# Tables of the first batch group in two passes: keys first, then values from a second reading of x, with joint rows moved to the second group and a new order

## Chip, core and metric

The kernel runs on one core of a Trainium2 chip. The metric is device time in microseconds. The kernel before was run nine times: median 2289.28 us, lowest 2274.66, highest 2302.47. The profile comes from one further execution of 2278.17 us. The engines are TensorE (PE, matrix products and transposes), VectorE (DVE), ScalarE (ACT), GpSimd (POOL, which also issues the indirect DMAs: gathers and scatters by row index) and SyncE (SP, which issues the plain DMAs in its queue's order).

## What is computed

Two graph layers over x (8 batches, 2048 nodes, 256 features) with one adjacency matrix (2048 x 2048, about 5 to 24 neighbours a row). Layer 0 is attention with 4 heads over the neighbours, with a softmax in each chunk of 256 nodes, then two normalizations. Layer 1 is graph attention with a softmax over all neighbours. Cut to what matters:

```python
q, k, v = (x @ W.T + b for each of Wq, Wk, Wv)            # 4 heads of 64
scores = clip(einsum('bhnd,bhjcd->bhnjc', q, kc) / 8, -10, 10)   # j: 8 chunks of 256 nodes
scores = where(mask == 0, -10, scores)
attn = softmax(scores, axis=-1)                            # within each chunk
ctx = einsum('bhnjc,bhjcd->bhnd', attn, vc)
x = layernorm(x + layernorm(ctx @ Wo.T + bo + x) * gamma + beta)
Wh = x @ W                                                 # layer 1
e = leaky_relu(s_src + s_dst); alpha = softmax(where(adj, e, -inf))
x = layernorm(x + elu(alpha @ Wh))
```

Since masked neighbours keep a weight of exp(-10) in each chunk, the kernel subtracts the chunk's mean of x before the value product ("centring"), so that the masked part becomes a constant that is added elsewhere. That is why values need the sum over a chunk of x, and keys do not.

## The kernel before, in words

**Sparse path.** Nodes are sorted by degree into 16 tiles of 128 nodes. Tile t has CAPS[t] neighbour slots (24, 14, 13, 12, 11, 11, 10, 10, 9, 9, 8, 8, 7, 7, 6, 5: 164 in all). The 8 batches are two groups of 4 (p = 0 and 1, "first" and "second"). One table row holds a node for all 4 batches of a group: 1024 numbers, 4 KB.

**Lists** (`edge_lists`). The adjacency rows are read, the neighbour numbers of each node are picked (L369, L406 to L412 on DVE), the nodes are ranked by degree (L378 to L397), each record is scattered to its place (L417, 16 indirect DMAs on POOL) and read back in order (L421). The index lists `idx`, `idk` (2 x index) and `idv` (2 x index + 1) are made from it (L429 to L435).

**Tables** (`tables(p, c2, ...)`, 8 chunks of two tiles of 128 nodes for each group). SP loads x (L699, 512 KB), PE transposes it (L682), ACT empties the bank with a running sum into `xs` (L705), POOL (first group) or DVE (second) adds beta (L708), and SP writes that to `xd_d` (L714). Then the chunk's mean is made (L722, L724), x is centred into `xc` (first group: one addition on POOL, L733; second group: 8 activations on ACT, L729), PE makes keys from `xT` and values from `xc` (L742, 32 matmuls of 256 columns a tile), DVE empties the keys with the bias (L747), ACT the values (L752), and SP writes both halves of the row of `kv_d[p]` (L754, L755), an 8 KB row of keys and values. Banks: the first group uses room "n" (two banks), which is given to the attention once the group's tables are done; the second group uses "m" (two banks), which transposes and queries use too. `shifts(p)` makes a constant of the query path from the sums of x (L760 to L789).

**Layer 0** (`layer0(v, p, t)` for each tile and group). `fetch_x` gathers x rows (L934); `query` transposes them (L682, ACT L945) and makes q (L953, L688). Keys are gathered (`gather`, L851, one indirect DMA a slot; two slots share a buffer of the room "u"), multiplied by q on DVE (L972), turned on PE (L985), copied by ACT (L988) and summed by heads on PE (L992), or reduced on DVE (L977) for the few units in `DOTS`. `softmax0` (L1007 to L1026) follows. Values are gathered (L851, by `idv`) and weighed (L894 on DVE for one or two slots at once, or L885 on ACT: 16 activations a slot), and summed by PE (L903). Some slots come as a joint row of key and value (`gather_both`, L864): S % 2 + 2 x COMBO[p] of a tile's S slots. With COMBO = (1, 0) that is 40 slots of the first group and 8 of the second. `apart0` says which slots go to ACT: the first SHARE[S] joint ones. `finish0` does the output product, the normalizations and the rows of layer 1.

**Layer 1** (`layer1`) gathers the new rows (L851), weighs (L894, L885) and sums (L903), for the two groups apart in 8 tiles and jointly in the other 8, and scatters the result (L1183).

**Order.** Every operation is put into a list with its engine, an estimated cost, its reads and writes and a due value v (`pl.stage(lo, hi)` spreads a range over the operations since the last call). When the program is built, `Plan.schedule` plays the list through: whenever an engine is free it takes the ready operation with the least v whose buffers are free. The result is each engine's fixed order; on the chip each engine goes through its own order and waits by semaphores. The due values are constants at the head of the file: WHENT (first value and step by chunk for the second group's tables), FIRST[0:2] the same for the first group's, WHEN0 the offsets of layer 0's steps, ORD0 and ORD1 the place of each tile. In the units of v, tile k of the first group stands at about k. Before, the second group's eight chunks stand at -22.35, -17.3, -12.25, -7.2, -2.15, 2.9, 7.95 and 13.

## Time and profile before

| what | value |
|---|---|
| profiled execution, time / span | 2278.17 us / 2276.4 us |
| PE, PE weight loads, DVE, ACT, POOL busy | 80%, 71%, 78%, 48%, 55% of the span |
| instructions | 36611 |
| DMA | 635.55 MB, mean 279 GB/s |
| gathers and scatters (queue q0) | 505.18 MB, 62.7% of 16 engines' span |
| plain DMAs (queue q1) | 126.24 MB, 15.1% |
| DVE busy by stage: 0 to 201, 201 to 361, 350 to 1000 us | 127.4, 84.2, 538.4 us |
| PE busy by the same stages | 153.7, 132.2, 558.1 us |

How to read the profile: a line of the groups has the source line, engine, operation, what is written and read, the count, then the busy time and mean duration, then the time the engine sat idle just before and what ended it. In a timeline the first two numbers are the start and the duration in us, and the bracket is the idle time before, with what ended it; "issue" is idle time that nothing in the profile explains. The slices on the page cut the span into 40 parts and give the busy share in tenths. The chain of work that ended last reaches back only to 1747 us in this profile; what happens before is read from the stages and the waits.

### The profile page before, as it was taken

What the parts mean: (1) busy time and instruction counts of PE and PEld (TensorE: products, weight loads), DVE (VectorE), ACT (ScalarE), POOL (GpSimd) and SP (SyncE); (2) the same over time, 40 slices, a digit from 0 to 9 for tenths busy, and PEclk for the clock granted to TensorE, in tenths of its full rate; (3) what the DMA queues carried; (4) which work ended last, traced back from release to release, by engine and by line L of the source; (5) the groups of instructions that cost most, each with busy time, mean ns of one, the idle gap of its engine ahead of it and who ended that gap; (6) DMA issues with size and microseconds to landing.
All of it is one profiled execution on the core that took longest, in us unless ns stands there. A gap on an engine that the chain in (4) does not pass through costs nothing. (4 is left out here: it accounts for less than half of the span.)

```text
span 2276.4 us, 36611 instructions
## 1 busy us (share of the span) xinstructions
PE 1819.2 (80%) x12215; PEld 1622.8 (71%) x12215; DVE 1766.6 (78%) x3262; ACT 1101.9 (48%) x4033; POOL 1249.0 (55%) x1192
## 2 busy tenths in 40 slices
PE   5697898788889788888787788888898867755755
PEld 4576788687778677777677777777787666755745
DVE  7922749698879777987777867788878788987987
ACT  6543544165355345441061532434455468664667
POOL 6684126554443434356646655555566565665676
PEclk9898999799989889999899988999999988877967
DMA  8867576898877767669868877888888699987873
GB/s 306 306 239 286 206 287 203 303 339 303 289 276 281 286 243 277 230 222 313 308 235 313 291 273 256 289 294 301 278 302 283 237 338 346 363 319 276 312 241 116
DMA packets 191672, 635.55 MB, mean 279 GB/s; under 512 B 36597, under 2 KB 54903, under 8 KB 178821
## 3 DMA queue, kind: packets, MB, share of 16 engines
q0 software_dynamic: 142160, 505.18, 62.7%
q1 hardware_dynamic: 46608, 126.24, 15.1%
q8 instruction: 99, 1.62, 0.3%
q10 hardware_dynamic: 2708, 1.71, 0.3%
q14 instruction: 97, 0.79, 0.1%
HBM read 596.19 MB, written 109.71 MB: 310 GB/s over the span
## 5 line engine op out<-in xcount | busy, mean ns | idle before, releaser
L903 PE MATMUL acc<-ident,u 128*128 128x128 f32 x2640 | 356.0, 288 | 57.4 <-DVE u L894 37.2
L903 PEld LDWEIGHTS acc<-ident,u 128*128 128x128 f32 x2640 | 321.2, 151 | 70.5 <-DVE u L894 42.6
L894 DVE TENSOR_TENSOR u<-u,h 128x2048 f32<-128x2048 f32 (+1 forms) x176 | 332.7, 1904 | 0.3
L972 DVE TENSOR_TENSOR u<-u,q 128x1024 f32<-128x1024 f32 x241 | 287.0, 1212 | 45.3 <-PE q L688 30.0
L851 POOL DMA_INDIRECT u<-kv_d,idv x194 | 211.2, 1089 | 195.4 <-PE acc L903 67.5
L851 POOL DMA_INDIRECT u<-kv_d,idk x206 | 208.5, 1012 | 193.8 <-issue 43.2
L885 ACT ACTIVATE u<-u,s 128x64 f32<-128x64 f32 x1056 | 261.1, 351 | 10.4 <-DVE s L1149 2.5
L985 PE MATMUL h<-ident,u 128*128 128x128 f32 x1568 | 209.2, 283 | 12.9 <-issue 7.6
L988 ACT COPY h<-h 128x256 f32<-128x256 f32 (+1 forms) x156 | 53.9, 346 | 323.4 <-PE h L985 169.2
L985 PEld LDWEIGHTS h<-ident,u 128*128 128x128 f32 x1568 | 186.7, 148 | 24.0 <-issue 11.4
L1082 PE MATMUL m<-wa,b 128*128 128x264 f32 x512 | 150.7, 430 | 27.7 <-issue 16.7
L821 ACT ACTIVATE b<-b,x,x 128x256 f32<-128x256 f32 x256 | 137.5, 602 | 72.5 <-DVE x L818 52.4
L1183 POOL DMA_INDIRECT out_dram<-b,nodeb x128 | 134.1, 1048 | 66.9 <-issue 28.6
L992 PEld LDWEIGHTS h<-sel,h 128*128 128x128 f32 x546 | 80.0, 202 | 117.1 <-ACT h L988 49.2
L903 PE MATMUL acc<-ident,at 128*128 128x128 f32 x1192 | 152.9, 278 | 8.4 <-issue 5.2
L992 PE MATMUL h<-sel,h 128*128 128x16 f32 x546 | 83.3, 261 | 94.5 <-ACT h L988 38.9
L894 DVE TENSOR_TENSOR at<-at,h 128x2048 f32<-128x2048 f32 (+1 forms) x82 | 154.3, 1890 | 2.3 <-DMA at<-kv_d,idv 2.2
L1052 PE MATMUL m<-wo,b 128*128 128x256 f32 x512 | 137.2, 392 | 20.1 <-issue 12.6
L953 PE MATMUL q<-wq,pair 128*128 128x256 f32 x512 | 140.0, 398 | 11.3 <-ACT pair L945 8.3
L903 PEld LDWEIGHTS acc<-ident,at 128*128 128x128 f32 x1192 | 137.6, 145 | 13.3 <-issue 7.3
L1082 PEld LDWEIGHTS m<-wa,b 128*128 128x128 f32 x512 | 98.2, 209 | 48.0 <-issue 20.4
L972 DVE TENSOR_TENSOR at<-at,q 128x1024 f32<-128x1024 f32 x87 | 103.7, 1212 | 31.0 <-PE q L688 20.5
(232 smaller groups left out, 4239.8 us busy)
## 6 DMA issues: line engine op xcount, KB each, us to landing
kv_d<-b SPq DMA_DIRECT2D x64, 512.0 KB
at<-in_adj_dram SPq DMA_DIRECT2D x16, 1024.0 KB
x_d<-b SPq DMA_DIRECT2D x32, 512.0 KB
b<-x_d SPq DMA_DIRECT2D x32, 512.0 KB
b<-in_x_dram SPq DMA_DIRECT2D x24, 512.0 KB
xd_d<-b SPq DMA_DIRECT2D x24, 512.0 KB
wj_d<-wh_d SPq DMA_DIRECT2D x16, 520.0 KB
at<-in_x_dram SPq DMA_DIRECT2D x8, 512.0 KB
```

The lines of the kernel that those rows point to most:

```text
L821: S(c_act(F, 2), lambda k=k: nc.scalar.activation(batches(dst)[:, k, :], src(k), AF.Identity, scale=rs.t[:, k:k + 1], bias=nm.t[:, k:k + 1 ...
L851: Pq(C_DGE, lambda u=u, o=o, s=s: nc.gpsimd.indirect_dma_start(out=flat(u)[:, o:o + size], out_offset=None, in_=table, in_offset=bass.Indi ...
L885: S(4 * C_WEIGH, lambda u=u, s=s, o=o, c=c, e=e, at=at: [nc.scalar.activation(flat(u)[:, o + h * D:o + (h + 1) * D], flat(u)[:, o + h * D: ...
L894: eng.tensor_tensor(pv, pv, av, op=ALU.mult)
L903: nc.tensor.matmul(quarters(accs[p][c // 4])[:, c % 4, :], flat(u)[:, o + c * P:o + (c + 1) * P], ident, is_transpose=True, start=not done ...
L953: nc.tensor.matmul(qb, cols(xT)[:, (2 * half + b) * KC + kc, :], wq[:, kc, :], start=(b == 0 and kc == 0), stop=False, skip_group_check=True)
L972: V(c_tt(GF), lambda u=u, o=o: nc.vector.tensor_tensor(by_feature(flat(u)[:, o:o + GF], "j b"), by_feature(flat(u)[:, o:o + GF], "j b"), b ...
L985: nc.tensor.matmul(pr.t[:, k * P:(k + 1) * P], flat(u)[:, o + j * P:o + (j + 1) * P], ident, is_transpose=True, start=(j == 0), stop=(j == ...
L992: nc.tensor.matmul(scv(s), prT.t[:, k * P:(k + 1) * P], sel, start=True, stop=True, skip_group_check=True)
L1052: nc.tensor.matmul(ob, cols(cT)[:, b * KC + kc, :], wo[:, kc, :], start=False, stop=(k == 1 and kc == KC - 1), skip_group_check=True)
L1082: nc.tensor.matmul(pw.t[:, 0:F + 2 * H], cols(xT1)[:, b * KC + kc, :], wa[:, kc, :], start=(kc == 0), stop=(kc == KC - 1))
L1183: Pq(C_DGE, lambda b=b: nc.gpsimd.indirect_dma_start(out=out_v[t * B + p * G + b], out_offset=bass.IndirectOffsetOnAxis(ap=nodeb.t[:, t, p ...
```

## The change

For the first group, `tables` now makes only the keys, from `xT`, and writes them to a table of their own, `k_d` (4 KB rows). A new function `again(0, c2)`, queued behind the keys with due values from -13.9 in steps of 0.25, reads x a second time, transposes it again, centres it on ACT while the bank is emptied, makes the values through room "m" and writes them to `v_d`. The chunk means are made on DVE. The second group keeps the joined table `kv_d` and its one pass; its chunks now stand at -4.0, -1.8, 0.4, 2.6, 4.8, 7.0, 9.2 and 11.4. COMBO becomes (0, 1): no joint rows in the first group, S % 2 + 2 in the second (40 slots). SHARE is given for each group, and the slots that go to ACT are the last ones of a tile, joint or not: 35 slots in the first group (29 before) and 11 in the second (7 before). The transposes of `query` now are ordered behind the group's shift. All other due values are new numbers.

```diff
-WHENT = (-22.35, 5.05)
+WHENT = (-4.0, 2.2)
-COMBO = (1, 0)
-SHARE = {5: 0, 6: 0, 7: 2, 8: 2, 9: 2, 10: 2, 11: 2, 12: 2, 13: 3, 14: 4, 24: 4}
+COMBO = (0, 1)
+SHARE = ({5: 0, 6: 0, 7: 3, 8: 2, 9: 3, 10: 2, 11: 3, 12: 2, 13: 3, 14: 2, 24: 2}, {5: 0, 6: 0, 7: 1, 8: 0, 9: 1, 10: 0, 11: 1, 12: 0, 13: 1, 14: 2, 24: 2})
...
-FIRST = (-38.1, 0.5, 2.25, -0.7, -40.65, -31.75, -38.15, -43.75, 4.9)
+FIRST = (-41.05, -0.7, 8.45, -1.45, -39.65, -25.25, -29.75, -38.6, 2.7)
+AGAIN = (-13.9, 0.25)
...
-    kv_d = [nc.dram_tensor(f"kv_d{p}", [N, 2 * GF], F32).ap() for p in range(NP)]
+    kv_d = nc.dram_tensor("kv_d", [N, 2 * GF], F32).ap()
+    k_d, v_d = (nc.dram_tensor(n, [N, GF], F32).ap() for n in ("k_d", "v_d"))
...
-        for t, xT, xc in both:
-            ks, vs = pl.new("b"), pl.new("b")
+        for t, xT in both:
+            keys(p, t, xT)
             if p:
+                xc = pl.new("l")
+                mean = got["mean", p, c2] if t % 2 else chunk_mean(p, c2)
                 for k in range(GK):
...
-            else:
-                Pq(60 + 2.35 * GF, lambda xT=xT, xc=xc: nc.gpsimd.tensor_tensor(
-                    cols(xc), cols(xT), mean.t[:, 0:GK].unsqueeze(2).to_broadcast([P, GK, P]), op=ALU.add), r=[xT, mean],
-                   w=[xc])
...
+                values(p, t, xc)
...
+    def keys(p, t, xT):
+        ks = pl.new("b")
+        project(xT, 0, "m" if p else "n", lambda b, pk: V(c_tt(512), lambda: nc.vector.tensor_tensor(
...
+        Q(lambda: nc.sync.dma_start((kv_d if p else k_d)[t * P:(t + 1) * P, 0:GF], rows(ks)), ROW, r=[ks], loose=[kk_b[p]])
+
+    def values(p, t, xc):
+        vs = pl.new("b")
+        project(xc, 1, "m", lambda b, pv: S(c_act(512), lambda: nc.scalar.copy(vs.t[:, b * F:(b + 2) * F], pv.t), r=[pv],
+                                            w=[(vs, b, b + 2)]))
+        Q(lambda: nc.sync.dma_start(kv_d[t * P:(t + 1) * P, GF:] if p else v_d[t * P:(t + 1) * P, :], rows(vs)), ROW, r=[vs], loose=[kv_b[p]])
+
+    def again(p, c2):
+        mean = chunk_mean(p, c2)
+        for t in (2 * c2, 2 * c2 + 1):
+            xl, xc, gate = pl.new("b"), pl.new("b"), pl.new("gx")
+            Q(lambda t=t, xl=xl: nc.sync.dma_start(batches(xl), x[p * G:(p + 1) * G, t * P:(t + 1) * P, :]
+                                                   .rearrange("b p f -> p b f")), ROW, w=[xl, gate])
+            for half in range(2):
+                pt = turned(xl, half)
+                for c in range(4):
+                    k = 4 * half + c
+                    S(c_act(P, 1), lambda c=c, k=k, pt=pt, xc=xc: nc.scalar.activation(
+                        cols(xc)[:, k, :], quarters(pt)[:, c, :], AF.Identity, bias=mean.t[:, k:k + 1]), r=[pt, mean, gate],
+                      w=[(xc, k, k + 1)])
+            values(p, t, xc)
...
     def apart0(p, t):
-        n = min(SHARE[CAPS[t]], len(got["both", p, t]))
-        return [items[0][0] for _, items in got["both", p, t][:n]]
+        n = SHARE[p][CAPS[t]]
+        return list(range(CAPS[t] - n, CAPS[t]))
...
-            pt = turned(xg, half)
+            pt = turned(xg, half, shift[p])
...
+    for c2 in range(NCH):
+        again(0, c2)
+        pl.stage(AGAIN[0] + c2 * AGAIN[1], AGAIN[0] + (c2 + 1) * AGAIN[1])
...
-        c = S_ - min(S_ % 2 + 2 * COMBO[p], S_)
-        halves_of = kv_d[p].rearrange("n (k f) -> (n k) f", k=2)
-        got["k", p, t] = gather(GF, halves_of, [kv_b[p]], idk, lambda s: idk.t[:, t, s:s + 1], list(range(c)), (p,), WW)
+        c = S_ - min(S_ % 2 + 2 * COMBO[p], S_) if p else S_
+        halves_of = kv_d.rearrange("n (k f) -> (n k) f", k=2)
+        of, at = (halves_of, idk) if p else (k_d, idx)
+        got["k", p, t] = gather(GF, of, [kk_b[p]], at, lambda s, at=at: at.t[:, t, s:s + 1], list(range(c)), (p,), WW)
...
-        got["v", p, t] = gather(GF, halves_of, [kv_b[p]], idv, lambda s: idv.t[:, t, s:s + 1], list(range(c)), (p,), WW)
+        of, at = (halves_of, idv) if p else (v_d, idx)
+        got["v", p, t] = gather(GF, of, [kv_b[p]], at, lambda s, at=at: at.t[:, t, s:s + 1], list(range(c)), (p,), WW)
```

`project(src, part, room, put)` holds the matmuls that stood in `tables` (four a bank, two banks a tile and part), and `chunk_mean` the two small DVE operations.

## The prediction

> **What bounds the kernel now.** I read the page first, then the busy time by stage, then the engines' timelines from 100 to 370 us, then who waited for whom. The page's slices (one is 56.9 us) name the place:
>
> ```profile
> PE   5697898788889788888787788888898867755755
> DVE  7922749698879777987777867788878788987987
> ```
>
> VectorE (DVE) stands nearly idle in slices 3 and 4 (114 to 228 us), while TensorE (PE) is at 80 to 90% there. Nothing like it comes again. The stages, with columns: length, then busy us (instructions) of PE, PE's weight loads, DVE, ACT and POOL, then the granted PE clock, DMA share and GB/s:
>
> ```profile
> 125.00:150.00 25.00, 24.04 (x121) 21.07 (x122) 5.01 (x8) 11.57 (x69) 19.61 (x16) 0.93 0.61 210
> 150.00:175.00 25.00, 25.00 (x125) 22.14 (x124) 5.04 (x8) 7.78 (x38) 22.31 (x24) 1.00 0.80 278
> 175.00:200.00 25.00, 23.94 (x122) 20.69 (x121) 9.22 (x31) 9.20 (x34) 4.58 (x5) 1.00 0.67 241
> 201.00:361.00 160.00, 132.18 (x751) 113.33 (x752) 84.18 (x95) 73.10 (x329) 51.21 (x50) 0.94 0.74 265
> 250.00:300.00 50.00, 47.53 (x273) 41.66 (x272) 33.48 (x37) 21.37 (x101) 9.02 (x9) 0.98 0.58 208
> 350.00:400.00 50.00, 45.91 (x342) 42.78 (x342) 46.41 (x37) 28.16 (x122) 34.91 (x23) 0.97 0.63 206
> 350.00:1000.00 650.00, 558.10 (x3680) 492.84 (x3680) 538.36 (x877) 302.69 (x1162) 309.14 (x295) 0.93 0.78 276
> 1000.00:1750.00 750.00, 626.46 (x4515) 567.65 (x4514) 586.25 (x997) 280.11 (x984) 430.80 (x420) 0.94 0.81 286
> ```
>
> From 125 to 200 us PE makes tables without a break and is the bound; DVE only empties banks. From 350 us on PE (558 of 650 us, 86%) and DVE (538, 83%) run side by side, neither full. POOL's timeline shows what opens the gathers, DVE's when they bear fruit:
>
> ```profile
> 175.53 0.96 POOL L417 DMA_INDIRECT rec_d<-b,x  x1 [0.30 <-issue]
> 183.89 1.13 POOL L934 DMA_INDIRECT pair<-xd_d,node  x1 [7.39 <-DVE node L437]
> ...
> 201.07 1.13 POOL L851 DMA_INDIRECT u<-kv_d,idk  x1 [13.18 <-DMA kv_d<-b]
> ```
>
> ```profile
> 239.89 1.22 DVE L972 TENSOR_TENSOR u<-u,q 128x1024 f32<-128x1024 f32 x1 [1.32 <-PE q L688]
> ...
> 360.74 6.69 DVE L894 TENSOR_TENSOR u<-u,s 128x2048 f32<-128x2048 f32 x3
> ```
>
> The lists are ready at 184 us, the first key row is asked for at 201 (the table's last write is awaited), the first product with a query comes at 240 (PE had a chunk of the second group's tables ahead of the query), and the first weighing of values at 361. In between PE makes 10 of the second group's 16 table tiles: 312 of their 512 matmuls lie at 200 to 350 us.
>
> **The change, part by part.** The sum is made against the profiled execution: 2278.2 us, span 2276.4.
>
> (1) Lists. The 16 record scatters (L417) run from 130.7 to 176.5 us on POOL, mixed with additions. The change takes the centring off POOL:
>
> ```profile
> L733 POOL TENSOR_TENSOR pair<-b,x 128x1024 f32<-128x1024 f32 x16 | 30.2, 1901 | 0.4
> ```
>
> Six of these (11.5 us) and three pairs of small ones (1.4 us) lie among the scatters, so the lists come 13 us earlier, at 171. From both sides: not at all (184; DVE now gets keys earlier, ahead of the ranks), or at 159 (16 scatters at 1.3 us from 130.7, and the same 7.4 us behind them). The key table costs PE 121.1 us / 2 = 60.5 us for half of the matmuls done before 201 us. Of the 153.7 us that PE was busy by then 93 remain, so keys stop being the gate. First key gather: 171 in place of 201; lead 30 us, bounds 17 and 42.
>
> (2) First gather to first weighing, now 160 us with 132 us of PE. 87 us of that are second-group tables (76.2 for the 312 matmuls, and 10 x 8 transposes at 1.04 us for eight); 45 stay. In their place comes the values pass: 60.5 us of matmuls and 16 x 1.04 = 17 us of new transposes, 77 us. By 171 us PE has 171 - 93 = 78 us free; some 45 of those lie before 125 us (PE is busy 80 there), when x is not all there, so about 30 us of the pass are done. Left are 47 + 45 = 92 us. At this stretch's own density (83%) that is 111 us, 49 less than 160; at the 95% of 250 to 300 us, 97. With none of the pass done ahead, 122 / 0.83 = 147, 13 less. New transposes, values and queries now share the two "m" banks, so I take 35. Lead at the first weighing: 30 + 35 = 65 us, bounds 30 and 105.
>
> Elsewhere in this pass: ACT gets 128 centrings at 0.30 us (4.81 us for 16, L729) = 39 us, some from a bank at 0.38; ACT is busy 73 of 160 us there, so they are covered, unless a bank waits for them. SP gets 16 more loads of 512 KB. That is 8.4 MB, 32 us of DMA at 265 GB/s; the stretch reached DMA share 0.74, and 21 MB of second-group traffic leave it, so I charge nothing. Without that cover it is 32 us, the other end.
>
> (3) The debt. Those 10 second-group tiles now start at the first tile's time and run among the attention of the first group: PE +87 us, DVE 10 x (1.22 + 2 x 0.69) = 26 us, DMA 21 MB. The stage from 350 to 1000 us then asks PE for 645 us. What it costs hangs on the density PE reaches. Table work waits for x alone and fills holes: where it ran beside scores, PE stood at 95% (250 to 300) and 92% (350 to 400). At 93.5% the stage takes 690 us, +40. At 98% (the tables alone, 125 to 200) 658, +8. At the stage's present 86% 750, +100. If DVE set the pace: (538 + 26) / 0.83 = 680, +30. I take +40, the rows where both kinds of work are mixed.
>
> (4) Joint rows move. First group: 40 slots that came as one 8 KB row come as two of 4 KB, second group 32 fewer: 8 more gathers in all at 1.3 us on POOL, which is busy 309 of 650 us in the one stage and 431 of 750 in the other. A joint unit holds its buffer from the key gather to the weighing; that burden goes to the second group. Neither trace row prices a buffer, so 0, with 15 us to either side.
>
> (5) Weighing. 46 in place of 36 layer-0 slots go to ACT (16 activations of 0.35 us each: +56 us, on an engine busy 303 of 650 and 280 of 750). DVE: 126 pairs and 30 singles in place of 140 and 12, -14 x 2.28 + 18 x 1.215 = -10 us. DVE is not the term that ends the stage above, so I count nothing; end -10.
>
> (6) The new order. Its priorities only say what goes first; between stages it may win or lose some us. 0, with 15 to either side.
>
> Sum: -65 + 40 = **-25 us**, 2253 against the profiled run. The median of the nine runs, 2289.3, lies 11 us above that run; on it the forecast is **2264**.
>
> **Two rules of the skill.** PE's 558 us against DVE's 538 make PE the scarcer engine, so that work added to PE is the dear part. The Trainium skill, Perfetto Trace Analysis, "Identifying the Most-Contended Engine", says that matmul busy time misleads and weight-load time is to be used: 493 of 650 us, 76%, which puts DVE first and would make the debt +30 and the sum -35. The trace takes PE's side where it can: 25.00 of 25 us at 150 to 175, with eight matmuls of 256 columns every 1.73 us and no gap. Against the change speaks DMA: Bandwidth & Descriptors, "Specifications", with an HBM limit of some 358 GB/s per core: by it the second reading is an estimated 23 us wherever DMA binds, and the sum -2. Slices of this trace reach 383 and 398 GB/s.
>
> **Rivals.**
> - *The debt is paid in full (slower).* Place: 350 to 1000 us. PE's holes there are not free for tables: its waits at the sums (L992) for ACT's copies and DVE's reductions, 28 us, and 40 us of "issue" (both 400 to 1000 us) come from the planned order within a tile. Density stays near 86 to 88%: 645 / 0.87 = 741, +91, less 65 = +26, 2315 on the median (2324 at 86%). It decides from 645 / 715 = 90% downward. For it: 86% is what this stage showed with little table work in it. Against: 92% and 95% where there was more.
> - *The front doesn't get shorter.* Lists stay at 184, or the second reading crowds the key gathers; lead 30 to 50, debt 40: 2279 to 2299. For it: DMA share 0.80 at 150 to 175, and SP's queue in order, where writes wait for DVE and hold loads behind them. Against: share 0.61 and 0.67 around it.
> - *DVE sets the pace and the holes are filled.* Debt 8 to 30, weighing -10: -45 to -67, 2222 to 2244. For it: every stage after 1750 us has DVE ahead of PE (440 against 357 of 526). Against: DVE's long waits of 400 to 1000 us are for PE (query L688, sums L992).
>
> **Numbers.** Forecast, -11 to -45 (a win over 0.5%): 0.42. DVE's pace: 0.11. Front not shorter, within 0.5% (about what a measurement of this kernel can tell from no change): 0.20. Debt in full: 0.27. So faster 0.53, same 0.20, slower 0.27. The range leaves out the far half of the DVE case and the far third of the debt case: 2232 to 2316. The forecast's own is 2244 to 2278.
>
> **What would show it.** (1) the last L417 at about 163 us and the first key gather near 171, waiting for the lists and not for the table; (2) first weighing (L894 before) near 295; (3) PE at 92% or more from there to 1000 us with 16 tiles of second-group tables in it; the end of the first group's layer 0 some 25 us earlier. Wrong, if PE in that stage stays under 90%, if the first value gathers wait for the value table long after the weights are ready, or if the gain of the front is seen at 400 us and gone by 1000.

## The result, and the profile after

The change made the kernel slower. The median after is 2312.6 us (10 runs, 2297.9 to 2330.3) against 2284.2 us before (31 runs, 2270.8 to 2302.5); the ratio is 1.0125, 95% interval 1.0093 to 1.0157. The forecast was 2264. The profiled execution took 2303.9 us with a span of 2302.1; before it was 2278.2 and 2276.4, so profile against profile the change costs 25.7 us.

The kernel before took 2041 us in some sets of runs and 2255 to 2284 us in others, so each experiment is judged by its ratio to the kernel before in the same set, and the words "at 2041", "at 2255" and "at 2284" below say which set a time of an event is from.

The page's slices of the kernel after (57.6 us each; PE above, DVE below):

```profile
PE   5585889698888889998788888889888867775764
DVE  7950539788788888886858878887888678989886
```

DVE's trough in slices 3 and 4 is still there (5 and 0 in place of 2 and 2), and PE, which had 9 and 7 in them, now has 8 and 5. So the front has not been filled. The stages of the kernel after (length, then busy us and instructions of PE, weight loads, DVE, ACT, POOL, then PE clock, DMA share, GB/s):

```profile
175.00:200.00 25.00, 15.91 (x65) 11.89 (x65) 0.00 (x0) 9.41 (x30) 9.59 (x10) 0.86 0.38 120
200.00:225.00 25.00, 14.70 (x68) 11.35 (x66) 5.13 (x25) 10.70 (x38) 16.56 (x17) 0.89 1.01 344
225.00:250.00 25.00, 14.12 (x64) 11.58 (x65) 0.00 (x0) 8.87 (x28) 6.75 (x7) 0.70 0.66 240
201.00:361.00 160.00, 128.27 (x723) 110.41 (x721) 66.16 (x87) 74.66 (x268) 52.81 (x52) 0.90 0.72 259
350.00:1000.00 650.00, 568.77 (x3812) 506.19 (x3811) 541.17 (x870) 347.91 (x1384) 341.91 (x326) 0.97 0.83 293
```

From 175 to 250 us PE is busy 45 of 75 us; before, it was busy 24 of 25 in the first of these slices. From 201 to 361 us it has 128 us of work, against 132 before: what left this stretch was replaced. From 350 to 1000 us it stands at 568.8 of 650, 87.5%, where 92% or more was forecast. POOL's, DVE's and SP's timelines of the kernel after hold the events that the prediction named (start, busy time, instruction, and in brackets the idle time before it and what ended that):

```profile
186.37 0.97 POOL L418 DMA_INDIRECT rec_d<-b,x  x1 [0.30 <-issue]
...
207.82 1.01 POOL L880 DMA_INDIRECT u<-k_d,idx  x1 [0.30 <-DVE x L469]
...
312.93 1.00 POOL L880 DMA_INDIRECT u<-v_d,idx  x1 [49.51 <-DMA xd_d<-b]
314.23 1.00 POOL L880 DMA_INDIRECT u<-k_d,idx  x1 [0.30 <-issue]
```

```profile
252.50 4.62 DVE L1000 TENSOR_TENSOR u<-u,q 128x1024 f32<-128x1024 f32 x4 [41.34 <-PE q L692]
...
321.16 1.22 DVE L1000 TENSOR_TENSOR u<-u,q 128x1024 f32<-128x1024 f32 x1 [4.55 <-DMA u<-k_d,idx]
...
357.08 0.29 DVE L1035 TENSOR_SCALAR s<-h 128x128 f32<-128x128 f32 x1 [3.27 <-PE h L1020]
...
365.80 2.35 DVE L923 TENSOR_TENSOR u<-u,s 128x2048 f32<-128x2048 f32 x1
```

```profile
198.03 0.32 SPq L769 DMA_DIRECT2D v_d<-b  x1
198.65 0.37 SPq L422 DMA_DIRECT2D pair<-rec_d  x1
...
307.77 0.33 SPq L769 DMA_DIRECT2D v_d<-b  x1
```

The last scatter is at 186 instead of the forecast 163, the first key gather at 208 instead of 171, the first weighing at 366 instead of 295. Two new waits show. The load of the sorted records (L422) is issued 0.6 us after a write of the value table (L769) which stood ahead of it in SP's queue; the last scatter had been issued 12 us earlier. And POOL stops for 49.5 us ahead of the first value gather. The bracket there names a write of `xd_d`, because a wait is put down to whatever came last; by the kernel, a value gather waits for all writes of the value table (`kv_b`), and the last of these was issued at 307.8, 5.2 us before the gather. Before the stop 24 key rows are gathered, the first tile's; the second tile's first key gather stands behind it, at 314 us. DVE's products show the same: 24 by 287 us, the next at 321, when a key row of the second tile has landed. The step that opens the first tile's softmax for its last 8 slots (L1035, at 357 us) comes behind those products in DVE's order and waits for PE's sums of the scores (L1020), and the weighing comes behind the softmax.

Where the 25.7 us came from, by events of the two profiles, and of the same two kernels at 2041 (from the two reference runs below):

| us | before | after | before, 2041 | after, 2041 |
|---|---|---|---|---|
| lists ready | 184.6 | 204.3 | 186.8 | 195.2 |
| first key gather | 201.1 | 207.8 | 203.2 | 198.8 |
| first product with a query | 239.9 | 252.5 | 234.8 | 226.8 |
| last write of the value table issued | | 307.8 | | 279.6 |
| first value gather | 264.7 | 312.9 | 259.8 | 285.5 |
| first weighing | 360.7 | 365.8 | 357.2 | 337.0 |
| stretch from the first weighing to the end | 1915.7 | 1936.3 | 1681.9 | 1719.7 |

So the change is a sum of two terms, as forecast. **Front:** 5 us lost in the profiles, 20 us won at 2041; forecast was 65 won. **Behind it, the debt:** 20.6 us in the profiles, 37.8 at 2041; forecast was 40. In the profiles 18 of the 20.6 us lie before the first group's last row is written (1053 us before, 1076 after); behind it the two kernels are within 3 us of each other.

### The profile page after: what moved, and what is told of

Same layout as the page of the kernel before. It is cut to its first block, busy times and chain, and to the rows that moved or that the text cites. A ratio compares the mean times of both kernels' runs of the same rounds, so it can differ in the third digit from the quotient of the medians.

```text
span 2302.1 us, 37253 instructions
## 1 busy us (share of the span) xinstructions
PE 1848.8 (80%) x12313; PEld 1645.1 (71%) x12313; DVE 1774.5 (77%) x3286; ACT 1166.7 (51%) x4323; POOL 1220.5 (53%) x1168
## 5 line engine op out<-in xcount | busy, mean ns | idle before, releaser
L932 PEld LDWEIGHTS acc<-ident,u 128*128 128x128 f32 x2800 | 331.1, 147 | 64.0 <-DVE u L923 33.3
L1000 DVE TENSOR_TENSOR u<-u,q 128x1024 f32<-128x1024 f32 x223 | 263.5, 1214 | 96.7 <-PE q L692 74.4
L914 ACT ACTIVATE u<-u,s 128x64 f32<-128x64 f32 x1216 | 302.5, 345 | 25.0 <-DMA u<-v_d,idx 8.3
L880 POOL DMA_INDIRECT u<-v_d,idx x115 | 121.2, 1054 | 154.9 <-DMA xd_d<-b 49.5
L1013 PE MATMUL h<-ident,u 128*128 128x128 f32 x1432 | 191.1, 283 | 10.5 <-DVE u L1000 2.7
L932 PE MATMUL acc<-ident,at 128*128 128x128 f32 x1248 | 173.2, 290 | 22.4 <-DVE at L923 17.5
L1013 PEld LDWEIGHTS h<-ident,u 128*128 128x128 f32 x1432 | 170.6, 148 | 19.7 <-DVE u L1000 5.5
L932 PEld LDWEIGHTS acc<-ident,at 128*128 128x128 f32 x1248 | 154.5, 152 | 28.1 <-DVE at L923 19.7
L880 POOL DMA_INDIRECT u<-k_d,idx x113 | 117.7, 1042 | 104.5 <-DVE h L1005 31.1
L1020 PEld LDWEIGHTS h<-sel,h 128*128 128x128 f32 x540 | 79.0, 202 | 92.6 <-ACT h L1016 38.0
L686 PE MATMUL m<-ident,b 128*128 128x128 f32 x576 | 97.2, 304 | 55.5 <-ACT b L767 18.3
L1020 PE MATMUL h<-sel,h 128*128 128x16 f32 x540 | 82.8, 261 | 71.2 <-ACT h L1016 30.1
L750 PE MATMUL m<-wkv,b 128*128 128x256 f32 x512 | 126.7, 400 | 13.4 <-issue 8.9
```

The costliest lines, as they stand in the source:

```text
L880: Pq(C_DGE, lambda u=u, o=o, s=s: nc.gpsimd.indirect_dma_start(out=flat(u)[:, o:o + size], out_offset=None, in_=table, in_offset=bass.Indi ...
L914: S(4 * C_WEIGH, lambda u=u, s=s, o=o, c=c, e=e, at=at: [nc.scalar.activation(flat(u)[:, o + h * D:o + (h + 1) * D], flat(u)[:, o + h * D: ...
L932: nc.tensor.matmul(quarters(accs[p][c // 4])[:, c % 4, :], flat(u)[:, o + c * P:o + (c + 1) * P], ident, is_transpose=True, start=not done ...
L1000: V(c_tt(GF), lambda u=u, o=o: nc.vector.tensor_tensor(by_feature(flat(u)[:, o:o + GF], "j b"), by_feature(flat(u)[:, o:o + GF], "j b"), b ...
L1013: nc.tensor.matmul(pr.t[:, k * P:(k + 1) * P], flat(u)[:, o + j * P:o + (j + 1) * P], ident, is_transpose=True, start=(j == 0), stop=(j == ...
L1020: nc.tensor.matmul(scv(s), prT.t[:, k * P:(k + 1) * P], sel, start=True, stop=True, skip_group_check=True)
```

## The experiments

Four theories: **late lists** (the list chain was planned late, on shared queues), **slow value pass** (no value row can be gathered until the whole value table is written, and that pass is long), **debt as one engine's work** (PE's matmuls or DVE's additions of the 6 tiles of second-group tables that moved behind the first weighing), and **debt from the rest of the change** (joint rows, ACT's larger share, the new order).

### The two kernels on one chip

No edit. 

> The changed kernel unaltered, as the reference of the runs of this study on the chip that they share (the kernel before takes 2041 us on the chip of the first four runs and 2284 on that of the two profiles). On the chip of the two profiles the change is 1.0125 [1.0093, 1.0157]. If the cost of the change is work of PE, DVE and the queues, the ratio here is 1.009 to 1.016. If it is DMA (a chip that moves data faster has less of it), it is below 1.008.

> The kernel before unaltered, for its trace on the same chip. In the two profiles the stretch from the first weighing to the end is 1915.7 us before and 1936.3 after (the debt, 20.6), and the first weighing comes at 360.7 before and 365.8 after (the front, 5.1). Four variants of the changed kernel with different fronts took 1723 to 1728 us for that stretch. If lead and debt are separate terms, the stretch here is 10 to 30 us shorter than in the changed kernel.

Measured: after 1.0095 (1.0078 to 1.0112), 2058.5 against 2040.7 us. The stretch behind the first weighing is 37.8 us longer, more than the 10 to 30 expected, and the first weighing 20.2 us earlier. The cost is much the same as at 2284, but its parts are not. The stage from 350 to 1000 us at 2041, the kernel before first:

```profile
350.00:1000.00 650.00, 602.88 (x4256) 543.35 (x4254) 597.99 (x950) 320.01 (x1230) 366.33 (x341) 0.98 0.85 313
```

```profile
350.00:1000.00 650.00, 609.95 (x4296) 550.60 (x4294) 587.34 (x955) 377.54 (x1486) 373.32 (x357) 1.00 0.87 316
```

Here PE reaches 93.8% in the changed kernel, next to the 93.5% of the forecast; the kernel before stands at 92.8%, though.

### Do the lists set the front?

**The list chain put ahead of all.** The planned order stays, but the chain's operations are placed right behind what each needs:

```diff
+def hoisted(order, some):
+    at, slots = {}, {}
+    for k, o in enumerate(order):
+        at[o] = float(k)
+        if o in some:
+            held = [at[p] for b in o.bufs for p, c in slots.get((b.pool, b.slot), ()) if c is not b]
+            at[o] = max([0.0] + held + [at[p] for p in o.deps]) + 1e-4
...
+    return sorted(order, key=at.get)
...
-        for o in self.schedule():
+        for o in hoisted(self.schedule(), self.early):
```

`early` holds the counts and ranks, the scatters, the load of the records and the list arithmetic; in the second run also the first three tiles' x rows and queries.

> The changed kernel, with the chain that makes the lists (counts, 16 scatters, the load of the sorted records, the list arithmetic) taken out of the planned order and put right behind what each step needs; nothing else is moved. In the changed kernel the lists are ready at 204 us, the first key gather is at 208, the first weighing at 366, and the time is 1.0125 of the kernel before. Theory 'late lists' (the front was lost because the list chain was planned late): lists near 180, first key gather near 182, first weighing 20 to 25 us earlier (341 to 346), ratio 1.002 to 1.005. Theory 'slow value pass' (the value table, done at 308 us, holds the first value gather and, in POOL's queue behind it, later key gathers): lists and first key gather come just as early, but the first value gather stays at 300 to 313 and the first weighing moves by less than 10 us; ratio 1.009 to 1.014.

> The changed kernel with the list chain moved as in the run above and, besides, the gather of the rows of x and the query (transposes, matmuls) of the first group's first three tiles put right behind what they need, ahead of the value pass on PE. Late lists: the first product with a query comes at 190 to 205 instead of 252, the first weighing at 320 to 340, ratio 0.995 to 1.003. Slow value pass: the first product comes that early too, but the value table is then done no earlier (308 or a few us later, PE's work is only exchanged), the first value gather follows it, the first weighing stays within 10 us of 366, ratio 1.009 to 1.016.

Measured: 1.0273 (1.0250 to 1.0295) and 1.0338 (1.0316 to 1.0361), both worse than the change. Lists came at 172 and 169 us, as asked, but the key table's last write slid to 198 and 196 (163 in the changed kernel), the first key gather came at 203 and 200, the first weighing at 373 and 385. Both theories missed the price of the move. The waits of the first of the two from 95 to 205 us tell it (waiting engine, tile and line, whom it waited for: us in total, times, longest; lines are 16 or 17 higher than in the kernel after):

```profile
PE h L767 <- ACT b L726: 27.3, 7, 12.3
...
ACT same L470 <- DVE s L463: 21.7, 1, 21.7
...
DVE s L446 <- DMA pair<-rec_d: 17.4, 1, 17.4
```

The list arithmetic of DVE waits for the records, ACT's casts (L470) wait for DVE's arithmetic, ACT's copies for the key tiles (L726) stand behind those casts, and PE waits for the copies. As each engine goes through its own order, what waits for the lists must not stand ahead of the key table.

**The same, with the shared queues eased.**

```diff
-                Pq(60 + 2.35 * GF, lambda add=add: add(nc.gpsimd), r=[be_b], w=[xl])
+                Pq(60 + 2.35 * GF, lambda: None, r=[be_b], w=[xl])
...
-    Q(lambda: nc.sync.dma_start(recv(srt), rec_d.rearrange("(t p) r -> p t r", p=P)), ...
+    Q(lambda: nc.gpsimd.dma_start(recv(srt), rec_d.rearrange("(t p) r -> p t r", p=P)), ...
```

> The changed kernel with the list chain moved as in the first experiment (lists ready at 172 us instead of 195, but the last write of the key table at 198 instead of 163), and with what it then stood in the way of taken off the shared queues: POOL's 16 additions of beta to the first group's rows are left out (35 us of POOL; these residual rows lack beta), and the sorted records are loaded on POOL's own queue, behind the scatters, instead of SP's. If lists and key table compete for POOL and SP, and the lead is worth its time: lists at 165 to 175, last key write at 163 to 175, first key gather at 172 to 180, first weighing at 310 to 322, ratio 0.997 to 1.003. If PE's own work sets the front: first key gather that early, but the first weighing at 330 or later, ratio 1.006 or more.

Measured: 1.0227 (1.0182 to 1.0272). Lists at 165, but the last key write still at 191, first key gather at 196, first weighing at 368. So easing POOL and SP does not bring the key table back. In this run's trace PE still waits 29.7 us for ACT's copies (L726) from 95 to 205 us and ACT's casts (L470) 16.5 us for DVE's arithmetic: the place in line on ACT and DVE is what is left, and the next run gives it up.

**Lists early with nothing in the way.** Counts and ranks together when the degrees are there, three scatters into each gap of POOL, the load on POOL's queue; DVE's list arithmetic at the earliest behind the last key addition, ACT's casts and the rest where they were planned.

```diff
+        if o in sets["counts"]:
+            t = 0.0
+        elif o in sets["scatters"]:
+            adds = sorted(at[a] for a in sets["adds"] if at[a] > last(sets["rank"]))
+            t = adds[min(len(sets["done"]) // 3, len(adds) - 1)]
...
+        elif o in sets["lists"]:
+            t = max(t - EARLY, last(sets["keys"]))
+        elif o in sets["first"]:
+            t -= EARLY
```

`first` is empty in the first run and holds the first tile's query, scores and softmax in the second; EARLY is 22 us.

> The changed kernel with three moves and nothing left out. The counting matmuls and ranks are taken together as soon as the degrees are there (in the changed kernel they are spread between key tiles, ranks at 168 us); the 16 scatters go three at a time into the gaps between POOL's additions behind them; the sorted records are loaded on POOL's queue. Unlike the first experiment nothing that waits for the lists is put ahead of the key table on PE, DVE, ACT or SP. Expected: lists at 168 to 178 us (195 in the changed kernel), last key write at 162 to 170, first key gather at 172 to 182. If the late lists set the front: first weighing at 312 to 322 instead of 337, ratio 0.997 to 1.003. If the first tile's query, which stands behind eight value tiles in PE's order, and the value table set it: first product no earlier than 220, first weighing at 330 to 337, ratio 1.006 to 1.010.

> As the run above, and the first tile's query, scores and softmax moved 22 us earlier in the planned order of all engines, ahead of four value tiles. If order alone holds the first tile: first product at 200 to 210 us instead of 227, first weighing at 312 to 325, ratio 0.997 to 1.004. If the front is held by the value pass, which then ends later by what went ahead of it (value table at 282 to 292 us instead of 280, first value gather behind it): first weighing at 330 or later, ratio 1.006 or more.

Both ran at 2255; the nearest uncut profile, at 2284, stands beside them. In the first, lists came at 182.6 (204.3 there), the last key write at 170.8 (162.5) and the first key gather at 185.8 (207.8), but the first weighing only at 359.8 (365.8); ratio 1.0081 (1.0046 to 1.0116). Two lines of POOL's timeline and one of DVE's in that run:

```profile
185.84 1.02 POOL L922 DMA_INDIRECT u<-k_d,idx  x1 [0.30 <-DVE x L507]
...
303.41 0.99 POOL L922 DMA_INDIRECT u<-v_d,idx  x1 [48.06 <-PE m L792]
```

```profile
359.78 2.29 DVE L965 TENSOR_TENSOR u<-u,s 128x2048 f32<-128x2048 f32 x1
```

The lists' 22 us are lost again in front of the value gather: POOL stops for 48 us as before. With the first query ahead as well the value table is done later (327.6 us), the first weighing comes at 382.9, and the ratio is 1.0224 (1.0181 to 1.0267). So late lists cost little: by these two profiles some 6 us of the 71 that the first weighing is late, and by the ratios (1.0081 against 1.0125, intervals that overlap) some 10 us of the whole.

### Does the value pass set the front?

**The pass left out.**

```diff
+        begun = len(pl.ops)
         again(0, c2)
+        for o in pl.ops[begun:]:
+            o.fn = lambda: None
...
-        of, at = (halves_of, idv) if p else (v_d, idx)
+        of, at = (halves_of, idv) if p else (k_d, idx)
```

> The changed kernel without its second pass: second reading of x, transposes, centring, value matmuls and the writes of the first group's value table are left out (77 us of PE), and the first group's values are gathered from the key table instead; the order of all that stays is untouched, the lists are as late as in the changed kernel. Slow value pass: the first value gather follows the free buffers at about 265 us, POOL's stop of 49.5 us goes, the first weighing comes at 300 to 325, and the end falls by 40 to 75 us against the changed kernel (ratio 0.980 to 0.995). Late lists: the first weighing stays at 345 or later, and the end falls by less than 25 (ratio 1.002 or more).

Measured: 0.9881 (0.9859 to 0.9903). First key gather 186.6, first product 194.9, first weighing 287.7 us: 49 us earlier than in the changed kernel at 2041, and the end 43 us earlier. The slow value pass was expected to give 40 to 75 us. As the pass's work on PE, ACT and SP is gone too, this prices the pass as a whole and not its last write alone.

**A quarter of the bytes read; half of the matmuls.**

```diff
-            Q(lambda t=t, xl=xl: nc.sync.dma_start(batches(xl), x[p * G:(p + 1) * G, t * P:(t + 1) * P, :]
+            Q(lambda t=t, xl=xl: nc.sync.dma_start(batches(xl)[:, 0:1], x[p * G:p * G + 1, t * P:(t + 1) * P, :]
```

```diff
-                    for kc in range(KC):
+                    for kc in range(kcs):
...
+                                            w=[(vs, b, b + 2)]), KC if p else 1)
```

> The changed kernel with the second reading of x cut to a quarter of its bytes (2.1 MB instead of 8.4; each transpose takes the quarter that was loaded, so PE, ACT and the writes do as much as before; the first group's values are then those of one batch of four). If the value pass is slow because the DMA is crowded (20 key gathers, 16 reloads and 16 writes in 100 us): the value table is done 10 to 30 us earlier than 308, the first weighing with it, ratio 1.000 to 1.008. If it is slow because each tile waits its turn for a buffer, a bank and a place in the queues: the table is done within 8 us of 308 and the ratio stays at 1.010 to 1.015.

> The changed kernel with half of the matmuls of the first group's value pass left out (only the first half of the inner dimension; these values are wrong): 30 us of PE in the front, everything else as it was. If PE's work sets the front: value table done at 252 to 265 us instead of 280, first weighing at 312 to 325 instead of 337, ratio 0.997 to 1.004. If the pass is held by reloads, banks and buffers that wait in turn: value table within 8 us of 280, first weighing at 332 or later, ratio 1.006 to 1.011.

Measured: 1.0083 (1.0052 to 1.0114), value table at 282.0, first weighing 336.3; and 1.0048 (1.0026 to 1.0070), table at 273.9, first weighing 331.7. The uncut kernel has 279.6 and 337.0. From the first to the last write of the value table it is 107.4 us uncut, 107.2 with a quarter of the bytes, 105.0 with half of the matmuls. So neither three quarters of the bytes nor half of the matmuls takes more than 2.4 us off the length of the pass at 2041, although the second cut takes PE from 98.0 busy us of 109 to 77.4 of 106 there. Part of the second run's gain was lost again, as its timelines show, ACT first, then PE:

```profile
194.88 3.56 ACT L454 CAST same<-s 128x368 bf16<-128x368 f32 x16 [8.24 <-DVE s L447]
198.34 1.05 ACT L767 COPY b<-m 128x512 f32<-128x512 f32 x2
```

```profile
198.96 0.19 PE L472 MATMUL m<-ones,x 128*1 128x1 f32 x2 [11.14 <-ACT b L767]
```

The faster pass ran into the lists: ACT's casts of the lists stand between two value tiles, the value copies (L767) behind them, and PE waits 11.1 us. In the uncut kernel at 2041 the same place costs 2.8 us. So that PE's work has no part in the length is not shown.

**What ties the first weighing.** In all 13 runs with a value pass (eight are in the table), whatever was moved or left out, the first value gather follows the last write of the value table by 3.5 to 6.1 us, and the first weighing follows the first value gather by 48 to 57 us (in the kernel before by 94 to 97 with the second group's tables and 73 without):

| run | last value write | first value gather | first weighing | weighing minus gather |
|---|---|---|---|---|
| after, 2041 | 279.6 | 285.5 | 337.0 | 51.5 |
| list chain ahead of all | 315.7 | 321.6 | 372.8 | 51.2 |
| and the queries | 329.2 | 334.4 | 384.5 | 50.1 |
| quarter of the bytes | 282.0 | 287.3 | 336.3 | 49.0 |
| half of the value matmuls | 273.9 | 280.0 | 331.7 | 51.7 |
| after, profile | 307.8 | 312.9 | 365.8 | 52.9 |
| lists early, 2255 | 298.2 | 303.4 | 359.8 | 56.4 |
| and the first query, 2255 | 327.6 | 331.1 | 382.9 | 51.8 |

That is the gate. The 48 to 57 us are the chain that the timelines above show: the second tile's key gathers behind the first value gather on POOL, that tile's products, and only then the rest of the first tile's softmax on DVE. The second group's tables, which PE makes in the same stretch, are not the reason: with their work left out (below) it is 51.4 us. No run took the second tile's gathers out of this place, so what another order would save is not known. And at 2041 the lead counts one for one, within 10 us: the stretch from the first weighing to the end took 1719.7, 1722.6, 1723.4, 1725.7, 1718.5, 1727.7 and, with no pass at all, 1728.3 us in the seven runs that leave the second group's tables alone, with first weighings between 288 and 385 us. Above 2041 this can't be read so closely: the profiled executions of the last three rows lie 8.7 us below, 10.5 above and 5.9 below the medians of their runs.

### What is the debt?

**Half of the second group's table matmuls left out, in both kernels.**

```diff
-                    for kc in range(KC):
+                    for kc in range(kcs):
...
+            r=[pk, kb_b], w=[(ks, b, b + 2)]), 1 if p else KC)
...
+                                            w=[(vs, b, b + 2)]), 1 if p else KC)
```

> The changed kernel with half of the matmuls of the second group's tables left out (only the first half of the inner dimension is summed, so the second group's keys and values are wrong; loads, transposes, DVE's additions and writes stay). In its profile 384 of these 512 matmuls lie behind the first weighing, and 0.24 us each, half of them is 46 us of PE. Debt as PE work: the stretch from the first weighing to the end falls by 25 to 45 us, and by at least 8 us more than in the kernel before with the same cut. Debt from the new order, the moved joint rows or transfers: the stretch falls by less than 15 us, and by about as much in both.

> The kernel before with the same half of the second group's table matmuls left out. Here 192 of the 512 lie behind the first weighing; half of them is 24 us of PE. Debt as PE work: the stretch from the first weighing to the end falls by 12 to 24 us, the first weighing comes up to 35 us earlier (some 150 matmuls less in front of it), ratio 0.975 to 0.985. Debt from order, joint rows or transfers: the stretch falls by less than 15 us, no less than in the changed kernel.

Measured: 1.0062 (1.0045 to 1.0079) and 0.9931 (0.9906 to 0.9956). What they won lies in front of the first weighing (329.9 instead of 337.0, 346.6 instead of 357.2). Behind it, the stretches are 1722.9 and 1681.6 us against 1719.7 and 1681.9 uncut. One line each, of the stage table of the changed kernel and of the cut one, from the first weighing to the end:

```profile
337.00:2056.70 1719.70, 1499.41 (x10946) 1368.66 (x10944) 1567.25 (x2881) 993.32 (x3662) 1079.80 (x1022) 0.95 0.87 321
```

```profile
329.90:2052.80 1722.90, 1476.19 (x10748) 1339.29 (x10746) 1567.43 (x2880) 991.51 (x3661) 1079.58 (x1021) 0.94 0.87 321
```

PE has 23 us less busy time (the expectation counted on 46) and the stretch is not shorter. Debt as PE's work, my own term, falls at 2041, and with it the reading that a PE at 93.8% is what ends this stage.

**DVE's additions left out, in both kernels.**

```diff
-                V(c_tt(GF), lambda add=add: add(nc.vector), r=[be_b], w=[xl], two=True)
+                V(c_tt(GF), lambda: None, r=[be_b], w=[xl], two=True)
```

> The changed kernel without the 16 additions of beta to the rows of the second group that VectorE makes in the table stage (the residual rows of that group lack beta). In the changed kernel on this chip 12 of them, 14.4 us, lie between the first weighing and the end of the first group's layer 0, in a stretch of 642 us with DVE busy 581 (before: 5 of them, 6.1 us, in 607 us with DVE busy 562). Half of the tables' matmuls of PE took nothing off either stretch. Debt as DVE work: the stretch from the first weighing to the end falls by 10 to 18 us (1720 to 1702 to 1710), ratio 1.000 to 1.005. Debt from order, joint rows or ACT's larger share: it falls by less than 5, ratio 1.007 or more.

> The kernel before without the same 16 additions. Debt as DVE work: the stretch from the first weighing to the end falls by 4 to 8 us (1682 to 1674 to 1678) because only 5 of them lie there; the others lie in front of the first weighing, where DVE waits; ratio 0.995 to 0.998. Debt from order, joint rows or ACT's larger share: less than 3 us.

Measured: 1.0040 (1.0018 to 1.0063) and 0.9959 (0.9937 to 0.9980); the stretches are 1713.3 (6.4 less) and 1677.7 (4.2 less). DVE's additions are part of it, 2 us of the difference of 38, and not the 10 to 18 us less in the changed kernel that this theory wanted.

**Both cuts.** 

> The changed kernel with both cuts at once: half of the matmuls of the second group's tables left out (46 us of PE behind the first weighing) and the 16 additions of beta to that group's rows left out (13 us of DVE there). Alone the first took nothing off the stretch from the first weighing to the end (1723 against 1720) and the second 6 us. If PE and DVE bind in turn, each hiding the other: the stretch falls by 18 to 35 us, 1685 to 1702, and the ratio is 0.990 to 0.997. If the debt is neither's work (order, buffers, the first group's gathers): it falls by 3 to 10 us, the ratio is 1.000 to 1.004.

Measured: 1.0056 (1.0031 to 1.0080) at 2255, above both expected ranges. Uncut it is 1.0125 at 2284 and 1.0095 at 2041; at 2255 the changed kernel was not run uncut. The two cuts alone were worth 0.3% and 0.6% at 2041, together 0.4 or 0.7% by the value taken: how they add up can't be read, but the wide gain of engines that bind in turn is not there.

**The first group's joint rows given up, in the kernel before.**

```diff
-COMBO = (1, 0)
+COMBO = (0, 0)
...
-        n = min(SHARE[CAPS[t]], len(got["both", p, t]))
-        return [items[0][0] for _, items in got["both", p, t][:n]]
+        n = min(SHARE[CAPS[t]], CAPS[t] % 2 + 2 * (1 - p))
+        return list(range(CAPS[t] - n, CAPS[t]))
```

> The kernel before with one part of the change alone: the first group's joint rows are given up (the 32 slots whose keys and values came as one row come in two gathers), ACT weighs as many slots as before, tables and the planner's numbers stay. The prediction counted this at nothing, 15 us to either side. If it is part of the debt: first weighing within 4 us of 357, the stretch from there to the end 1692 to 1706 instead of 1682, all of it before the first group's last row is written (964 us), ratio 1.005 to 1.012. If it costs nothing: the stretch within 4 us, ratio 0.998 to 1.002.

Measured: 0.9973 (0.9950 to 0.9995). It costs nothing: a kernel that leaves nothing out, 0.3% under the kernel before. The second group's new joint rows and ACT's larger share were not tried alone.

**No engine's work for the second group's tables, transfers and order kept, in both kernels.** The buffers that then hold old data are set to zero at the start.

```diff
             tables(p, c2, v0 + c2 * dv, v0 + (c2 + 1) * dv)
+            for o in pl.ops[begun:] if p else ():
+                if o.eng != "SP":
+                    o.fn = lambda: None
```

> The changed kernel without any engine's work for the second group's tables: transposes, ACT's copies and centring, matmuls, DVE's additions are left out for all 16 tiles (the second group's tables then hold old data), while every transfer of that stage (x in, tables and residual rows out) stays, and so does the order of all that is left. In the changed kernel 12 of the 16 tiles lie behind the first weighing, in the kernel before 6. If the debt is the table work as a whole (banks, ACT's copies and hand-offs, of which PE's matmuls and DVE's additions alone are little): the stretch from the first weighing to the end falls by 35 to 75 us here and by 15 to 40 in the kernel before with the same cut, and the two stretches are within 10 us of each other (uncut they differ by 38 us on a fast chip and 21 on a slow one). If it is the new order, ACT's larger share of the weighings, the gathers or the transfers: the two stretches still differ by 18 us or more.

> The kernel before without any engine's work for the second group's tables, transfers kept, as in the run above. Ten of those tiles lie in front of the first weighing here. If they are what the front waits for: the first weighing comes at 290 to 315 us instead of 357, and if the debt is table work the stretch behind it falls by 15 to 40 us; ratio 0.955 to 0.975. If order, ACT's share, gathers or transfers make the debt: the stretch behind it falls by no less than in the changed kernel and stays 18 us or more shorter than there.

Measured at 2255: 0.9984 (0.9951 to 1.0017) and, in only four executions, 0.9819 (0.9756 to 0.9882). The stretches from the first weighing to the end, changed kernel first:

```profile
355.80:2242.30 1886.50, 1496.86 (x10480) 1354.73 (x10480) 1544.83 (x2832) 929.47 (x3351) 1077.11 (x1023) 0.90 0.82 292
```

```profile
320.00:2206.60 1886.60, 1492.45 (x10488) 1344.46 (x10488) 1544.04 (x2823) 890.39 (x3183) 1055.28 (x1017) 0.91 0.80 283
```

1886.5 and 1886.6 us, where 20.6 us (37.8 at 2041) lay between the two uncut. The first of these executions lies 7.1 us below the median of its runs, the second at its median, so the agreement is good to some 7 us. The debt needs engines' work for those tables: without it, everything else of the change (order, joint rows, 39 us more of ACT, transfers) adds no more than some 7 us to this stretch. Whether the rest would cost something beside the tables is not shown. How far each stretch fell can't be read exactly, as the uncut profiles are from a set in which the kernel before took 30 us more (2284). In front, the kernel before gained 41 us here (first weighing 320.0 for 360.7; 290 to 315 was expected), while the changed kernel's first weighing stays at 355.8 behind a value table done at 300.7: of its front (365.8 and 307.8 at 2284) at most some 10 us are held by the second group's tables.

## Why the prediction was wrong

**The step that failed is (2), from the first gather to the first weighing, and with it (1): the lead was put at 65 us and was -5 in the profiles and 20 at 2041.** The debt, the other large term, came to 37.8 us at 2041 and to half of the forecast's 40, 20.6, in the profiles. Of the 51 us between -25 and +25.7, the lead makes 70 and the smaller debt takes 19 back.

- *(1) Lists.* Forecast 171 us, found 204 (195 at 2041). I took the centring additions off POOL and moved the scatters up, but their start is set by the ranks, and the new order counts between key tiles on PE: the ranks are at 167 instead of 130 us. Then the record load waited in SP's queue behind a value write. "Keys stop being the gate" was right: the key table's last write is at 162 us and the first key gather waits for lists. That they can be earlier was shown too (182.6 at 2255), but 22 us of it are worth some 6 at the first weighing.
- *(2) First gather to first weighing.* Forecast 124 us, measured 158 (138 at 2041). I added up PE's work and divided by a density. I let ten second-group tiles (87 us of PE) leave this stretch; the traces show ten in front of the first weighing before and four after, so six left. And a value gather may touch any row, so none can start before the last of 16 value tiles is written, and 48 to 57 us follow from there to the first weighing in every run, as POOL's and DVE's orders put part of the second tile in between. I had listed "first value gathers wait for the value table" as a sign of failure and had no term for it. The pass itself takes 107 us at 2041 and 136 in the profile where PE's part is 77.
- *(3) The debt.* Forecast 40, measured 20.6 and 37.8. That 37.8 is near 40 is luck: I had 87 us more of PE's work behind the first weighing, the traces have 47.6 (35.9 at 2041), and half of the matmuls left out changed nothing at 2041. It comes with the table work as a whole. In the profile PE's share in the stage was 87.5%, the value for which I had worked out +91; the rival "the debt is paid in full" read the density rightly and its price wrongly. Its 2315 us is 2 from the median by luck: it had a lead of 65 and a debt of 91.
- *(4), (5), (6)* were set to nothing, and without the table work they come to no more than some 7 us together.
- *The rivals.* "The front doesn't get shorter" named the right place, with lists at 184 and writes in SP's queue that hold loads; it still allowed a lead of 30 to 50. Its end, 2299, was 14 us short of the median. "DVE sets the pace" was nearer than PE's density at 2041: the stretch did not move with PE's work and moved 6 us with 13 us of DVE's. What I set against it was misread: DVE's longest wait from 400 to 1000 us before is not for PE but for "issue" (24.0 us, the row at the end).
- *The two rules.* From 350 to 1000 us at 2041 PE leads by matmul time (610.0 us, DVE 587.3) and is behind DVE by weight-load time (550.6); that half of the table matmuls could go for nothing speaks for the second order: PE was not the scarce one. Weight-load time is one of the two measures that the Trainium skill, Perfetto Trace Analysis, "Identifying the Most-Contended Engine", asks for on PE (the other is the rate of useful arithmetic). The 30 us that it made of the debt lie between the two measured values, my 40 above both. DMA: Bandwidth & Descriptors, "Specifications", priced the second reading at an estimated 23 us, so three quarters of it at an estimated 17. Left out, they brought 0.1% (2 us) at 2041, and the two intervals leave room for some 10 us, so that price is not seen. The kernel after also has a stretch above that page's 358 GB/s:

```profile
325.00:350.00 25.00, 22.47 (x128) 19.48 (x127) 13.19 (x15) 9.26 (x45) 10.96 (x11) 0.93 1.03 411
```

**Open.** Which of the table work's parts makes the debt: DVE's beta additions are 2 of 38 us, half of PE's matmuls none; ACT's copies, DVE's key additions (8 us more in the stretch) and the two shared "m" banks were not tried one by one. Also why the value pass takes 107 us, as three quarters of the bytes and half of the matmuls are no more than 2.4 us of it; that its tiles stand in PE's and ACT's order between list casts, queries and sums of the first tile is shown at one place (11.1 us) and only argued for the rest.

## What to carry to other kernels

A stage that gathers by index from a table, any row of which may be asked for, starts when the last row is written; so a lead is worked out from that one event and the chain behind it, not from the sum of the work in front. When a pass is split in two, look for the end of its second half: here the first weighing followed that and not the early keys. And where each engine keeps its own order, earlier is not better by itself: here the list chain, moved ahead of its data, held the key table back by 35 us.

## What was not expected of the hardware

The kernel before, in the same order, has a span of 2276.4 us in the profile and 2039.1 in the reference run, with DVE busy 1766.6 and 1762.4 us and PE 1819 and 1754. Most of the difference is idle time. Summed over the trace's waits, PE stood 148 us for "issue" (nothing that the profile shows) in the first and 4 in the second, DVE 135 for "issue" and "remote" against 1, ACT 267 against 6. One row of each, of DVE's reductions of the first group's key products:

```profile
DVE h L977 <- issue: 24.0, 5, 7.9
```

```profile
DVE h L977 <- issue: 0.7, 1, 0.7
```

What causes it was not tried. The mean granted PE clock is 0.911 in the first and 0.941 in the second. It isn't the chip alone: the record has the same chip number beside 2041 and, later, beside 2255. It moved the terms of this change (front 25 us, debt 17) by about as much as the change's own net (25.7 and 17.6).
